# Moving the adjacency's transpose into the last stage of a two-layer decoder, with 47 blocks of rows and a woven last shared expert

## The chip, the cores and the metric

The kernel runs on one core of one Trainium2 chip. A core has TensorE (PE: matrix products, with its weight loads, PEld, beside them), VectorE (DVE), ScalarE (ACT), GpSimd (POOL) and SyncE (SP, which here only issues transfers). The DMA queues carry data between device memory (DRAM) and the on-chip memory (SBUF); PE writes into PSUM banks, from which DVE and ACT read. The metric is device time in microseconds (us), median over several runs of one launch.

## The reference

The input `x` holds 4 batches of 512 tokens with 512 dimensions; a context holds 4 x 512 rows of 128. Two layers follow one another, each step with a residual and a layernorm (all float32):

- layer 0: causal self-attention (16 heads of 32); cross-attention to the context (32 query heads of 16, 8 key heads); a feed-forward net with activations quantised to 8 bits and ternary weights;
- layer 1: causal self-attention; a mix with a learned adjacency; a mixture of experts.

The adjacency comes from the context alone, and is 512 x 512 for each batch:

```python
sim = jnp.einsum('bhnd,bhmd->bnm', Q, K) / (jnp.sqrt(jnp.float32(d)) * H)
k = max(1, int(n * TOP_K_RATIO))                       # 153 of 512
threshold = jax.lax.top_k(sim, k)[0][:, :, -1:]
A_learned = jax.nn.sigmoid(sim) * (sim >= threshold)
A_learned = (A_learned + jnp.swapaxes(A_learned, -1, -2)) * 0.5
return (1.0 - gamma) * adj_raw + gamma * A_learned     # adj_raw is the decoder's x here
```

The mixture of experts sends each of the 2,048 tokens to 2 of 16 experts (512 -> 256 -> 512 with silu and a gate), weights the two results, and adds one shared expert (512 -> 512 -> 512) that all tokens pass:

```python
for e in range(N_EXPERTS):
    h = jax.nn.silu(flat @ Wu[e]) * (flat @ Wg[e])
    out = out + combine[:, e:e + 1] * (h @ Wd[e])
out = out + jax.nn.silu(flat @ Su[s]) * (flat @ Sg[s]) @ Sd[s]
```

## The kernel before

Tokens lie on the 128 partitions: a batch is `X[b]`, 128 x 4 x 512 (NT = 4 tiles of rows). `ident` is the identity matrix, with which PE transposes 128 x 128 pieces into PSUM. The stages follow one another; times are those of the profile:

- 0 to 562 us: self-attention of layer 0. 562 to 1100: cross-attention. 1100 to 1400: feed-forward. 1400 to 1996: self-attention of layer 1. From 1973 on, overlapping its end: `experts`.

**Self-attention and the selection beside it.** In `self_attention` PE's instructions are chained in the order in which they are written (`in_order`, recorded at L424 for all of them; the adjacency's own lines keep their numbers). Between heads it calls `background()`, which advances a generator, `selecting(...)`, by one step. It computes the similarities of a batch (PE products L959 and L964, scaled into SBUF), finds each row's threshold (the 153rd largest) by repeated counting, and then runs `adjacency(b, s, pool)`, L986: a first loop makes the masked half-sigmoid of each row tile (ACT L990, DVE L991 and L993, all in place in the similarity tile `s[i]`), a second loop transposes four pieces per row tile into one PSUM bank (L999), adds the untransposed tile (DVE, L1001), and stores the sum into the DRAM tensor `mixed` (SP, L1002). Layer 0's self-attention carries batches 0 and 1, layer 1's carries 2 and 3. PSUM there is `psum(3, 1, 1)`: three pairs of banks, one bank for transposes (`psum_tp`), and one more. So a transpose group waits until the bank's last reader, a DVE or ACT instruction, is done.

**Cross-attention and the ternary weights.** `cross_attention` runs 135 passes of its inner loop. It calls `background()` in the passes after 2 x NT, and in the passes t = 1, 3, 5, 7, 9, 11 besides; every second call advances the ternary quantisation of the feed-forward weights by one step (51 steps: a load on SP, L681, with DVE work such as L687 behind it). The first passes also issue three DMAs on SP that zero `xs` (L659).

**Experts.** Here no order is pinned: the scheduler of the language orders each engine's instructions from the order of emission and its own estimates. PSUM is `psum(2, 2, 2)`: two pairs, two banks for transposes, two more.

1. For each batch: `mix_adjacency(b, ap)` loads the four row tiles of `mixed` (two buffers `adj`) and adds them to the scaled residual on DVE (L1117); `layernorm` (L105 statistics, L106, ACT root L108, L110, L112 scaling); `transposed` makes `xT` (PE L122, copies on DVE L126 and ACT L124, 16 transposes per batch); `route(b)` does the router (PE L1171, L1179, a chain of small DVE operations L1180 to L1215, ACT's exponent L1188).
2. Counts over all tokens (PE, L1258 to L1269), a chain on DVE that turns them into a position for each (token, choice), and 32 POOL scatters (L1318) that write the rows of `X` into `xs` in DRAM, sorted by expert and padded to blocks of 128 rows.
3. `shared(b, acc)`: in two halves, up and gate products (PE L1226), silu (ACT L1231), product `sh` (DVE L1232), down products (PE L1237) and DVE additions (L1243) into `acc[b]`. It is emitted for batches 0 to 2 after the scatters, and the scheduler puts much of it into PE's gaps of steps 1 and 2; batch 3 is emitted after the blocks (L1384).
4. Blocks: 16 rounds of 3 streams (`LS` = 16, `NS` = 3), block j = s x 16 + k. Each loads its expert's weights on SP if they are new in its stream (L1344, L1349), its 128 rows `xb` (L1353, three buffers), transposes them (L1358, copy L1360), and runs the products (L1363, silu L1368, `h` L1370, transposes L1373, copy L1375, down L1377, copy L1382, store into `ys` on ACT's queue L1383). At most `NB` = 47 blocks can be filled; all 48 of the 3 x 16 run.
5. Return: for each tile of tokens two POOL gathers from `ys` into `yg` (L1390, four buffers), weighted and added on DVE (L1394); then `layernorm` of the batch and its store (SP, L1399).

Of the kernel before, what the change touches and what calls it, by code (L numbers as in the profile page):

```python
# [13 lines left out]
F32 = mybir.dt.float32  # L14
# [3 lines left out]
ALU = mybir.AluOpType  # L18
# [3 lines left out]
P = 128  # L22
B, S, D = 4, 512, 512
NT = S // P
# [16 lines left out]
def decoder_kernel(ctx: ExitStack, tc: tile.TileContext, a: dict, out: bass.AP):  # L41
    nc = tc.nc
    V, A, G, T = nc.vector, nc.scalar, nc.gpsimd, nc.tensor
# [17 lines left out]
    def psum_tp(dt=F32, n=4):  # L61
        return ps["tp"].tile([P, n, P], dt, tag="tp", name="tp")
# [5 lines left out]
    ident = const.tile([P, P], F32, tag="ident", name="ident")  # L68
# [22 lines left out]
    for b in range(B):  # L91
        xb = const.tile([P, NT, D], F32, tag=f"x{b}", name=f"x{b}")
# [7 lines left out]
    def layernorm(b, x=None):  # L100
        x = X[b] if x is None else x
        st = small.tile([P, NT, 6], F32, tag="bst", name="bst")
        mv = small.tile([P, NT, 2], F32, tag="bmv", name="bmv")
        for i in range(NT):
            V.bn_stats(st[:, i, :], x[:, i, :])  # L105
            V.bn_aggr(mv[:, i, :], st[:, i, :])  # L106
        sd = small.tile([P, NT], F32, tag="bsd", name="bsd")
        A.activation(sd, mv[:, :, 1], AF.Sqrt, bias=eps_t)  # L108
        rs = small.tile([P, NT], F32, tag="brs", name="brs")
        V.reciprocal(rs, sd)  # L110
        for i in range(NT):
            V.tensor_scalar(  # L112
                x[:, i, :], x[:, i, :], mv[:, i, 0:1], rs[:, i : i + 1],
                ALU.subtract, ALU.mult,
            )
# [358 lines left out]
    def cross_attention(background):  # L474
        HD, NG, NJ, NP = XD, XG, 4, XP
        multiply, transpose = in_order()
        with tc.tile_pool(name="ck", bufs=1) as kp, tc.tile_pool(
            name="cx", bufs=2
        ) as xp, tc.tile_pool(name="cpt", bufs=3) as pt, tc.tile_pool(
            name="co", bufs=2  # L480
# [5 lines left out]
            for k in range(2):  # L486
                KS.append(kp.tile([P, NG, S], BF16, tag=f"ks{k}", name=f"ks{k}"))
                KL.append(kp.tile([P, NG, S], BF16, tag=f"kl{k}", name=f"kl{k}"))
                t = kp.tile([P, NT, NG, 32], F32, tag=f"va{k}", name=f"va{k}")
                V.memset(t, 1.0)  # L490
                VA.append(t)
            for k in range(3):
                t = kp.tile([P, NT, NJ, 32], BF16, tag=f"xl{k}", name=f"xl{k}")
# [137 lines left out]
            p = o = end = None  # L631
            for t in range(NT * total + 7):
                (n, i), k, v = divmod(t, NT), t - 5, t - 6
                if n < total:
                    maxima(n, i, 0)
                late, p = p, softmax(*divmod(k, NT)) if 0 <= k < NT * total else None
                if late:
                    if v % NT == 0:
                        o = psum_mm()
                    values(*divmod(v, NT), o, late)  # L640
                    if v % NT == NT - 1:
                        end = finish(v // NT, o)
                        next(end)
                if n < total:
                    maxima(n, i, 1)
                if i == 0 and 0 < n <= total:
                    least(n - 1)
                elif i in (1, 2) and n + 1 < total:
                    turn(n + 1, i - 1)
                elif i == 3:  # L650
                    next(end, None) if end else None
                    if n + 2 < total:
                        split(n + 2)
                if t > 2 * NT:
                    background()
                if t < 12 and t % 2:
                    background()
                if i == 0 and 0 < n <= NS:
                    nc.sync.dma_start(  # L659
                        xs[ts(n - 1, LS * P), :].rearrange("(j p) d -> p j d", p=P),  # L660
                        zero.unsqueeze(1).to_broadcast([P, LS, D]),
                    )
# [316 lines left out]
    rest = const.tile([P, 1], F32, tag="rest", name="rest")  # L979
# [4 lines left out]
    mixed = tc.dram_tile([B * NT * P, S], F32, name="mixed")  # L984

    def adjacency(b, s, pool):  # L986

        for i in range(NT):
            e = pool.tile([P, S], F32, tag="y", name="y")
            A.activation(e, s[i], AF.Tanh, scale=0.5)  # L990
            V.tensor_scalar(e, e, quarter, quarter, ALU.mult, ALU.add)  # L991
            n = b * NT + i
            V.scalar_tensor_tensor(s[i], s[i], thr[:, n : n + 1], e, ALU.is_ge, ALU.mult)  # L993
            if i % 2:
                yield
        for i in range(NT):
            tp = psum_tp()
            for c in range(NT):
                T.transpose(tp[:, c, :], s[c][:, ts(i, P)], ident)  # L999
            u = pool.tile([P, S], F32, tag="y", name="y")  # L1000
            V.tensor_tensor(u, tp.rearrange("p c t -> p (c t)"), s[i], ALU.add)  # L1001
            nc.sync.dma_start(mixed[ts(b * NT + i, P), :], u)  # L1002
            if i % 2:
                yield

# [104 lines left out]
    def mix_adjacency(b, ap):  # L1110
        u = ap.tile([P, NT, S], F32, tag="adj", name="adj")
        nc.sync.dma_start(
            u, mixed[b * NT * P : (b + 1) * NT * P, :].rearrange("(t p) d -> p t d", p=P)
        )
        for i in range(NT):
            x = X[b][:, i, :]
            V.scalar_tensor_tensor(x, x, rest, u[:, i, :], ALU.mult, ALU.add)  # L1117
        layernorm(b)


# [5 lines left out]
    NB = (2 * B * S + NE * (P - 1)) // P  # L1126
    NS = 3
    LS = -(-NB // NS)
    NBP = NS * LS

    def experts(xs, ys):
        with tc.tile_pool(name="sims3", bufs=1) as sp:
            select_again(Similarities(sp))
        with tc.tile_pool(name="mx", bufs=1) as xp:
# [82 lines left out]
            def shared(b, acc):  # L1217

                for half in range(2):
                    h = xp.tile([P, F // P, S], F32, tag="sh", name="sh", bufs=2)  # L1220
                    for f in range(F // P):
                        col = ts(half * (F // P) + f, P)
                        pp = psum_pair()
                        for j, w in enumerate((swu, swg)):
                            for c in range(NK):
                                T.matmul(  # L1226
                                    pp[:, j, :], w[:, c, col], xT[b][:, c, :],
                                    start=(c == 0), stop=(c == NK - 1),
                                )
                        s = xp.tile([P, S], F32, tag="ss", name="ss", bufs=2)  # L1230
                        A.activation(s, pp[:, 0, :], AF.Silu)  # L1231
                        V.tensor_tensor(h[:, f, :], pp[:, 1, :], s, ALU.mult)  # L1232
                    for k in range(NT // 2):
                        po = psum_pair()
                        for i in range(2):
                            for f in range(F // P):
                                T.matmul(  # L1237
                                    po[:, i, :], h[:, f, ts(2 * k + i, P)],
                                    swd[:, half * (F // P) + f, :],
                                    start=(f == 0), stop=(f == F // P - 1),  # L1240
                                )
                        two = slice(2 * k, 2 * k + 2)
                        V.tensor_tensor(  # L1243
                            acc[:, two, :], po, (acc if half else X[b])[:, two, :], ALU.add
                        )

            with tc.tile_pool(name="adj", bufs=2) as ap:
                for b in range(B):
                    mix_adjacency(b, ap)
                    t = xp.tile([P, NK, S], F32, tag=f"xT{b}", name=f"xT{b}")  # L1250
# [72 lines left out]
                        tc.declare_no_dep(d.ins, e.ins, reason="rows of their own")  # L1323
                    sent.append(d)
            for b in range(3):
                shared(b, acc[b])

            with tc.tile_pool(name="mw", bufs=1) as wp, tc.tile_pool(name="mh", bufs=3) as hp:
                wug = [wp.tile([P, NK, 2, F], F32, tag=f"wug{s}", name=f"wug{s}") for s in range(NS)]
# [2 lines left out]
                for k in range(LS):  # L1332
                    for s in range(NS):
                        j = s * LS + k

                        with tc.issue_after(last.ins) if last else nullcontext():
                            e = nc.sync.value_load(ebi[0:1, j : j + 1], min_val=0, max_val=NE - 1)
# [43 lines left out]
                        yb = hp.tile([P, D], F32, tag="yb", name="yb")  # L1381
                        A.copy(yb, pp[:, 1, :])  # L1382
                        nc.scalar.dma_start(ys[ts(j, P), :], yb)  # L1383
                shared(B - 1, acc[B - 1])  # L1384
                for b in range(B):
                    for i in range(NT):
                        t = b * NT + i
                        for k in range(2):
                            y = hp.tile([P, D], F32, tag="yg", name="yg", bufs=4)
                            G.indirect_dma_start(  # L1390
                                out=y, out_offset=None, in_=ys,
                                in_offset=bass.IndirectOffsetOnAxis(pos[k][:, t : t + 1], 0),
                            )
                            V.scalar_tensor_tensor(  # L1394
                                acc[b][:, i, :], y, wt[k][:, t : t + 1], acc[b][:, i, :],
                                ALU.mult, ALU.add,
                            )
                    layernorm(b, acc[b])
                    nc.sync.dma_start(out[b].rearrange("(t p) d -> p t d", p=P), acc[b])  # L1399

    xs = tc.dram_tile([NBP * P, D], F32, name="xs")
    ys = tc.dram_tile([NBP * P, D], F32, name="ys")


    def selecting(batches, pool, before=()):
# [96 lines left out]
```

## Time and profile before

| | us |
|---|---|
| median of 3 runs (2554.65 to 2563.09) | 2555.62 |
| profiled execution, device time | 2553.13 |
| its span | 2551.4 |
| PE busy in the span | 2270.9 (89%) |
| DVE busy | 1431.1 (56%) |
| ACT busy | 1102.6 (43%) |
| POOL busy | 625.4 (25%) |
| counts done (PE) | 2041.8 |
| scatters | 2051.2 to 2093.4 |
| first block's products | 2169.3 |
| last product of the blocks | 2474.2 |
| first gather | 2482.3 |

1.7 us of the execution lie outside the span. A line of a group gives the source line, the engine, the operation and its tiles, the number of instructions, and their time. A row of the timeline gives start, length, engine and line, and in brackets how long the engine stood idle before it and whose end released it; rows of PE overlap a little, as its ends are modelled, so the time from one start to the next is the better measure of what an instruction takes. Idle time on an engine that does not bound a stage costs nothing there.

### The profile page before, as it was taken

To read this page: it belongs to the slowest core of one execution; us is meant where nothing else is said; L and a number is where in the kernel's file an instruction comes from. 1 tells how busy PE (TensorE), PEld (TensorE's weight loads), DVE (VectorE), ACT (ScalarE), POOL (GpSimd) and SP (SyncE) were. 2 spreads that over 40 slices of the span, in tenths; PEclk is the share of its full clock that TensorE was granted. 3 is DMA by queue.
4 is the path that set the end of the run, shared out by engine and by line. 5 is a ranking of instruction groups with operands and counts; after the bars stand their busy time and mean duration, and the time that the engine had idled before them with its cause. 6 is when DMAs were issued, how large, how long until landed. Compare 5 with 4: busy or idle time off the path is not lost. (4 is left out here: it accounts for less than half of the span.)

```text
span 2551.4 us, 34801 instructions
## 1 busy us (share of the span) xinstructions
PE 2270.9 (89%) x13032; PEld 1005.0 (39%) x13032; DVE 1431.1 (56%) x3138; ACT 1102.6 (43%) x1742; POOL 625.4 (25%) x1218
## 2 busy tenths in 40 slices
PE   7899889978989899989988689988999889999995
PEld 2334333333333233346555234433434334444442
DVE  2455555548888778758888445555555921111117
ACT  0732373225767677766665273246223200222211
POOL 7300020013333233136766240012000040000004
PEclk9899989889999999999999789998998999999997
DMA  6500000028221301000000200000001260434545
GB/s 220 155 1 18 17 1 1 1 72 308 83 83 53 114 17 34 1 1 1 1 1 1 85 1 1 1 17 1 1 1 53 83 222 17 145 119 155 179 123 186
DMA packets 93725, 164.27 MB, mean 64 GB/s; under 512 B 7408, under 2 KB 39536, under 8 KB 93552
## 3 DMA queue, kind: packets, MB, share of 16 engines
q1 hardware_dynamic: 76144, 123.20, 14.8%
q10 hardware_dynamic: 12288, 22.03, 2.3%
q0 software_dynamic: 5120, 16.78, 2.0%
q8 instruction: 103, 1.69, 0.3%
q14 instruction: 70, 0.57, 0.1%
HBM read 165.13 MB, written 51.90 MB: 85 GB/s over the span
## 5 line engine op out<-in xcount | busy, mean ns | idle before, releaser
L554 DVE TENSOR_REDUCE nm<-sc 128x2 f32<-128x1024 f32 x256 | 304.0, 1218 | 94.5 <-PE sc L424 94.0
L592 ACT ACTIVATE p<-sc 128x1024 f32<-128x1024 f32 x256 | 248.6, 1025 | 128.9 <-PE sc L424 128.7
L246 DVE CUSTOM_DVE_ANT_0 e<-sc,late_keys 128x256 bf16<-128x256 f32 (+3 forms) x512 | 223.3, 485 | 130.2 <-PE sc L424 130.1
L296 ACT ACTIVATE p<-sc 128x512 f32<-128x512 f32 (+3 forms) x256 | 166.0, 701 | 227.3 <-PE sc L424 227.2
L424 PE MATMUL mm<-p,va 128*32 128x512 f32 (+3 forms) x2048 | 215.1, 524 | 0.4 <-ACT oT L607 0.3
L1363 PE MATMUL sc<-wug,xbT 128*128 128x512 f32 x384 | 186.3, 599 | 14.9 <-ACT sl L1368 11.9
L424 PE MATMUL sc<-qs,ks 128*128 128x512 bf16 x512 | 147.4, 381 | 26.8 <-DVE nm L554 25.0
L424 PE MATMUL sc<-kT,qT 32*128 32x512 f32 (+3 forms) x1024 | 136.5, 501 | 25.0 <-ACT p L296 20.9
L424 PE MATMUL sc<-ks,qs 128*128 128x512 bf16 x512 | 155.3, 387 | 3.8 <-DVE nm L554 2.5
L324 DVE RECIPROCAL u<-u 128x128 f32<-128x128 f32 x128 | 108.4, 909 | 68.0 <-ACT u L311 68.0
L424 PE MATMUL sc<-qT,kT 32*128 32x256 f32 (+3 forms) x1024 | 130.8, 507 | 12.6 <-DVE st L246 10.8
L1390 POOL DMA_INDIRECT yg<-ys,pi x32 | 33.2, 1037 | 413.7 <-DMA ys<-yb 390.6
L1032 ACT ACTIVATE junk<-sim,mid 128x512 bf16<-128x512 f32 x176 | 125.2, 726 | 19.3 <-POOL mid L1025 19.3
L747 POOL TENSOR_TENSOR y<-z 128x512 f32<-128x512 f32 (+1 forms) x48 | 97.3, 2040 | 87.4 <-DVE z L732 87.3
L1360 DVE COPY xbT<-tp 128x512 f32<-128x512 f32 x48 | 32.9, 688 | 124.3 <-PE tp L1358 117.4
L1370 DVE TENSOR_TENSOR h<-sc,sl 128x256 f32<-128x256 f32 x48 | 20.2, 420 | 143.7 <-ACT sl L1368 143.7
L1363 PEld LDWEIGHTS sc<-wug,xbT 128*128 128x128 f32 x384 | 67.3, 190 | 81.7 <-issue 64.7
L424 PEld LDWEIGHTS sc<-kT,qT 32*128 32x128 f32 x1024 | 52.4, 189 | 115.1 <-issue 70.2
L747 POOL TENSOR_TENSOR z<-y 128x512 f32<-128x512 f32 x64 | 95.3, 1510 | 3.4 <-issue 2.1
L424 PEld LDWEIGHTS <-ks 128*128 128x128 bf16 x512 | 50.0, 98 | 104.3 <-issue 58.3
L1377 PE MATMUL sc<-wd,hT 128*128 128x512 f32 x192 | 90.2, 592 | 0.0
L424 PEld LDWEIGHTS sc<-qT,kT 32*128 32x128 f32 x1024 | 51.0, 193 | 92.7 <-issue 62.1
(297 smaller groups left out, 4202.5 us busy)
## 6 DMA issues: line engine op xcount, KB each, us to landing
wug<-in_Wu SPq DMA_DIRECT2D x48, 512.0 KB
wug<-in_Wg SPq DMA_DIRECT2D x48, 512.0 KB
wd<-in_Wd SPq DMA_DIRECT2D x48, 512.0 KB
xs<-zero SPq DMA_DIRECT2D x3, 4096.0 KB
xb<-xs SPq DMA_DIRECT2D x48, 256.0 KB
ys<-yb ACTq DMA_DIRECT2D x48, 256.0 KB
w<-in_w_gate SPq DMA_DIRECT2D x16, 512.0 KB
w<-in_w_up SPq DMA_DIRECT2D x16, 512.0 KB
```

The costliest lines, as they stand in the source:

```text
L246: V.tensor_tensor_reduce(e, at[r], late_keys[:, (NT - m) * P :], 1.0, LOWEST, ALU.add, ALU.max, accum_out=st[:, i, r : r + 1],)
L296: A.activation(heads, sc[h][:, :, :m], AF.Exp)
L324: V.reciprocal(sums[:, ts(i, P)], sums[:, ts(i, P)])
L424: ins = op(*args, **kw)
L554: V.tensor_reduce(NM[n][:, i, 2 * h : 2 * h + 2], sc, AX.X, ALU.max, negate=True)
L592: A.activation(p[:, 2 * h : 2 * h + 2, :], sc[h], AF.Exp)
L747: then(pool, getattr(G, op)(*args))
L1032: A.activation(e, s[k], AF.Sign, bias=bias[:, k : k + 1], accum_out=to[:, k : k + 1])
L1360: V.tensor_copy(xbT, tp)
L1363: T.matmul(pp[:, 0, :], xbT[:, c, :], wug[s][:, c, :, :].rearrange("p q f -> p (q f)"), start=(c == 0), stop=(c == NK - 1),)
L1377: T.matmul(pp[:, 1, :], hT[:, c, :], wd[s][:, c, :], start=(c == 0), stop=(c == F // P - 1),)
L1390: G.indirect_dma_start(out=y, out_offset=None, in_=ys, in_offset=bass.IndirectOffsetOnAxis(pos[k][:, t : t + 1], 0),)
```

## The change

- `cross_attention` no longer calls `background()` in the passes t = 1, 3, ..., 11.
- `adjacency` stores the masked tile `s[n]` itself into `mixed`, as soon as it is made. The second loop with its 64 transposes (over the four batches), 16 DVE additions and two yields per batch goes.
- `mix_adjacency` transposes the loaded tiles: 4 transposes per row tile (64 in all) into `psum_tp`, and one more DVE addition that reads them from PSUM (16 in all).
- `shared` becomes a generator that yields after each column of `sh` and each pair of down products (8 yields). For batches 0 to 2 it is run through at once. For batch 3 it is advanced once for two of every three token tiles between the gathers, and run to its end ahead of the last batch's gathers.
- The block loop skips j = 47, the last turn of its third stream; `ys` has 47 x 128 rows.
- The gathered rows use in turn the buffers `yg`, `xb` and `yb`, three each.

```diff
--- before.py
+++ after.py
@@ -653,8 +653,6 @@
                 if t > 2 * NT:
                     background()
-                if t < 12 and t % 2:
-                    background()
                 if i == 0 and 0 < n <= NS:
                     nc.sync.dma_start(
@@ -991,15 +989,7 @@
             V.scalar_tensor_tensor(s[i], s[i], thr[:, n : n + 1], e, ALU.is_ge, ALU.mult)
-            if i % 2:
-                yield
-        for i in range(NT):
-            tp = psum_tp()
-            for c in range(NT):
-                T.transpose(tp[:, c, :], s[c][:, ts(i, P)], ident)
-            u = pool.tile([P, S], F32, tag="y", name="y")
-            V.tensor_tensor(u, tp.rearrange("p c t -> p (c t)"), s[i], ALU.add)
-            nc.sync.dma_start(mixed[ts(b * NT + i, P), :], u)
+            nc.sync.dma_start(mixed[ts(n, P), :], s[i])
             if i % 2:
                 yield
@@ -1113,8 +1103,12 @@
         for i in range(NT):
+            tp = psum_tp()
+            for c in range(NT):
+                T.transpose(tp[:, c, :], u[:, c, ts(i, P)], ident)
             x = X[b][:, i, :]
             V.scalar_tensor_tensor(x, x, rest, u[:, i, :], ALU.mult, ALU.add)
+            V.tensor_tensor(x, x, tp.rearrange("p c t -> p (c t)"), ALU.add)
         layernorm(b)
@@ -1230,6 +1224,7 @@
                         V.tensor_tensor(h[:, f, :], pp[:, 1, :], s, ALU.mult)
+                        yield
                     for k in range(NT // 2):
@@ -1243,6 +1238,7 @@
                             acc[:, two, :], po, (acc if half else X[b])[:, two, :], ALU.add
                         )
+                        yield
@@ -1323,7 +1319,8 @@
             for b in range(3):
-                shared(b, acc[b])
+                for _ in shared(b, acc[b]):
+                    pass
@@ -1332,6 +1329,8 @@
                         j = s * LS + k
+                        if j == NB:
+                            continue
@@ -1381,12 +1380,19 @@
-                shared(B - 1, acc[B - 1])
+
+                rest = shared(B - 1, acc[B - 1])
                 for b in range(B):
+                    if b == B - 1:
+                        for _ in rest:
+                            pass
                     for i in range(NT):
                         t = b * NT + i
+                        if t % 3 != 2:
+                            next(rest, None)
                         for k in range(2):
-                            y = hp.tile([P, D], F32, tag="yg", name="yg", bufs=4)
+
+                            y = hp.tile([P, D], F32, tag=("yg", "xb", "yb")[(2 * t + k) % 3], name="yg")
@@ -1399,7 +1405,7 @@
-    ys = tc.dram_tile([NBP * P, D], F32, name="ys")
+    ys = tc.dram_tile([NB * P, D], F32, name="ys")
```

## Prediction

> **What bounds the kernel now.** I read the engine totals first, then busy time by stage, then the instructions that the diff touches, and last the waits around them on TensorE (PE), VectorE (DVE) and the gather queue (POOL).
>
> The first block is the page's busy line; the second is busy time by stage (columns: window, its length, then PE, PE weight load, DVE, ACT, POOL busy with instruction counts, granted clock, DMA share, GB/s).
>
> ```profile
> PE 2270.9 (89%) x13032; PEld 1005.0 (39%) x13032; DVE 1431.1 (56%) x3138; ACT 1102.6 (43%) x1742; POOL 625.4 (25%) x1218
> ```
>
> ```profile
> core 0: us, PE busy (x) PEld busy (x) DVE busy (x) ACT busy (x) POOL busy (x), PEclk, DMA share, GB/s
> 0.00:560.00 560.00, 500.94 (x3189) 207.41 (x3190) 279.00 (x823) 214.54 (x421) 96.32 (x320) 0.95 0.15 49
> ...
> 1400.00:1973.00 573.00, 509.03 (x3281) 216.52 (x3282) 290.55 (x839) 230.03 (x442) 85.13 (x292) 0.92 0.05 16
> 1973.30:2000.00 26.70, 16.51 (x59) 6.57 (x51) 26.70 (x59) 2.54 (x5) 0.58 (x3) 0.90 0.56 182
> 2000.00:2041.80 41.80, 41.80 (x177) 19.23 (x178) 36.57 (x190) 17.48 (x26) 0.00 (x0) 0.94 0.11 39
> ...
> 2169.45:2474.15 304.70, 285.64 (x839) 134.73 (x838) 48.85 (x93) 63.12 (x141) 0.00 (x0) 1.00 0.46 147
> 2474.15:2551.40 77.25, 47.77 (x103) 20.34 (x101) 49.26 (x93) 11.34 (x16) 33.17 (x32) 0.80 0.54 170
> ```
>
> PE bounds both self-attentions (89% busy) and the blocks (94%). The mixing stage is bound by DVE first (26.70 of 26.70) and then by PE (41.80 of 41.80). In the last 77 us no engine is full: gathers, DVE and PE wait for one another.
>
> The DVE add that follows the adjacency's transposes, with the waits behind it; then PE rows (start, length, work, idle before it and its releaser); then two gathers:
>
> ```profile
> L1001 DVE TENSOR_TENSOR y<-tp,sim x16: 648/692/693, 273.1 to 1951.3; 128x512 f32<-128x512 f32 x16
> ...
>   PEld tp L999: 7.3, 9
>   PE tp L424: 7.1, 4
>   PEld L424: 6.0, 2
> ```
>
> ```profile
> 277.71 0.46 PE L424 MATMUL tp<-ident,pm 128*128 128x128 bf16 x4 [2.00 <-DVE y L1001]
> ...
> 2096.28 1.33 PE L1358 MATMUL tp<-ident,xb 128*128 128x128 f32 x5 [10.89 <-DMA xb<-xs]
> ...
> 2494.92 8.78 PE L1237 MATMUL sc<-swd,sh 128*128 128x512 f32 x14 [4.08 <-DVE sh L1232]
> ```
>
> ```profile
> 2530.97 1.01 POOL L1390 DMA_INDIRECT yg<-ys,pi  x1 [5.77 <-DVE x L1394]
> 2534.73 1.21 POOL L1390 DMA_INDIRECT yg<-ys,pi  x1 [2.76 <-DVE x L1394]
> ```
>
> The reader is to see that L999 stands in PE's written order with one transpose bank, so that PE attention work waits for a DVE add; and that late gathers wait for buffers.
>
> **The change part by part**, against the profiled execution's own 2553.13 us (span 2551.40).
>
> *Self-attention loses 64 transposes and 16 adds.* PE rows around L999, next start minus start, give 2.44, 2.35, 2.08 and 3.2 us of work for the four batches: 10.1. The waits for L1001 are 2.00 + 1.36, 0.97, 2.35 and 1.36 + 0.15: 8.2. What PE gains is lost again where another engine is late next, the softmax's ACT or DVE. PE is busy 0.89 of these stages, so I count 0.89 of the work, 9.0, and two thirds of the waits, 5.5: **-14.5**. Bounds: -18.3 if all is kept, -5 if half the work alone is. The 16 stores stay on SP and go out earlier, right after each mask. The next batch overwrites the similarity tiles, so a late store could hold it; but the masks of a batch are made up to a hundred us ahead (L993 starts at 130, the transposes at 266), so this costs nothing. If that cover went, it would cost one store's landing, about 5 us by the adjacency's load (1987.73 to 1992.79), per batch. Two yields fewer per batch bring the next batch's selection two background calls forward on DVE, ACT and POOL, which changes their work's place and not its amount.
>
> *Cross-attention loses six background calls* (three weight steps and their loads: on SP the first two loads now stand behind two zeroings of `xs`, before one led them at 564.69 and SP stood 9.05 at the next, 567.00; `xs` is first needed at the scatters, 2051, the context's next loads at 607, so SP is no loser). One L687 step of 1.21 us at 582.32 stands in a stretch where DVE runs without a gap (573.1 to 586) and PE then idles 4.47 for DVE (586.39). The steps come back later, where PE is the bound and the 51 steps still end by pass 110 of 135. **-1**; bounds -3 (one DVE step each) and +2 (the three come back exposed, less the first).
>
> *The mixing stage gains 64 transposes, 16 adds from PSUM and table loads.* I walked the new order of PE, DVE and ACT with rows of before: transpose start to start 0.11 to 0.14, L1117 0.65, add 0.60 (L1001 start to start), statistics 0.59 + 0.09, scaling 0.46, copy of xT 0.60, the router's products 3.54. Batch b's mix transposes stand behind batch b-1's x transposes, and both use the same two PSUM banks. The routes end 2026.2, 2044.8 and 2064.9 for batches 1 to 3 (before: 2015.8, 2026.1, 2034.6), and the counts 30.0 later than 2041.8. But 24 more of the shared expert's products (24 x 0.858, each two passes of 0.43 = 20.6) now stand ahead of the counts and leave the stretch behind the scatters. Net +9.4: 48 of the transposes at 0.13 (6.2; the other 16 fit between the Wo groups), one wait of 4.4 of a shared product for `sh` (made at about 2036 behind the mixing on DVE), less 1.4 that batch 0's layernorm gains. That wait also costs clock: 14 products at 0.43 are 6.2 with the last one's end, and L1237 took 8.78 after an idle 4.08 and 7.78 (2097.40) after 10.89, so 1.6 to 2.6 more; I take 2.0, between them. **+11.4**. Bounds: +5 (transposes alone, less the 1.4) and +19 (16 adds exposed as well, 9.6). A gain is excluded: PE is busy 41.80 of 41.80 where most of this is put.
>
> [...]
>
> *47 blocks.* Steady blocks take 6.50 (2303.08 to 2329.06 for four), the first five 5.45, as their rows were transposed while PE waited. A block less is not 6.5 less: in the new order 15 row transposes (3.75 blocks) are made ahead of the first products, not 20 (five blocks), and from the 19th block on each block has one transpose of its successor and three of the one after in its gap. With products at 0.43, transposes at 0.11, and the waits last product to first of 1.43, 1.32 and 1.10 for four, three and one transpose between, the walk gives 302.6 before (trace: 304.9) and 299.2 after: **-3.4**. Bounds -6.5 and +2 (rows arrive late in some blocks: on a block that loads weights the rows' load lands 6.8 after the block's start and is wanted at 6.6).
>
> *Last expert woven, nine buffers instead of four.* Gathers run at 1.37 each when nothing holds them (first ten from 2482.26 = T). Before, they wait 16 us in all for buffers, 5.77 and 2.76 of it near the end, the last issues at T+55.3, and the last scaling L112 ends T+63.7. With nine buffers the last could issue at T+42.5, and landing (3.71, 2537.57 to 2541.28) and finish (4.66) would give T+50.9. DVE denies part of that: in its new order two `sh` stand behind up to seven gathered adds (0.66 each), L1237 waits for them, and the last batch's adds wait for L1237 and the two adds L1243 (1.22 each). The walk ends at T+56.9: **-6.8**. Bounds -12 (the gathers alone) and -2 (L1237 waits as before, 4.08 and 6.09). SP's output stores follow their batches as before; the gathers stay alone on POOL.
>
> *Sum:* -14.5 - 1 + 11.4 - 3.4 - 6.8 = -14.3, so 2553.1 - 14.3 = 2538.8 profiled. The median of the runs is 2555.62, 2.5 above the profiled execution, so I say **2541**.
>
> **Rivals.**
> - *Slower: the mixing stage goes serial.* Place: batch b's mix transposes (two banks) behind b-1's x transposes, with DVE full. My walk spaces the batches (2064.9 - 2026.2)/2 = 19.4 apart. With no overlap a batch is DVE 4 x (0.65 + 0.60 + 0.68 + 0.46) + 2 x 0.60 + about 5.0 of routing (2027.3 to 2033.5 less two other operations) = 15.8; PE 2.1 + 2.1 + 3.8; ACT about 5 (root 0.30, copy 0.57, exponent 0.26, three table loads of 1.28): 28.8. Three intervals 9.4 longer are +28: 2538.8 + 28 = 2567 profiled, 2569. It decides from 26.7 a batch ((14.3 + 7.7)/3 more). For it: DVE's 26.70 of 26.70. Against: the shared expert's products can fill PE's waits and are then not owed later.
> - *No difference: self-attention's time isn't PE's.* Only -5 comes there: -4.8 in all, 2551. For it: 11% of those stages PE waits on softmax. Against: the L1001 waits are followed by PE work at once.
> - *More gained:* all 18 in attention, +5 in the mix, -12 at the end: -18 - 1 + 5 - 3.4 - 12 = -29.4, so 2526. For it: gathers ran unheld for ten in a row. Against: DVE's order in the last stage.
> - *The 4.4 wait costs no clock:* the 2.0 falls away, 2536.8 profiled, 2539. For it: PE went on at full rate after idles of 2.35 and less. Against: the row with 4.08. [...]
> - *The 47th block saves nothing* (the diff doesn't do what it says for time): -10.9, so 2545. Some rhythm is lost for sure.
>
> **How the numbers follow.** Forecast 0.35 (own range 2532 to 2549, which holds the next too), no clock lost 0.15, serial mix 0.14, no difference 0.16, more gained 0.15, no block saved 0.05. 0.3% is 7.7 us, about what a measurement can tell here. Faster: 0.35 + 0.15 + 0.15 + 0.05 = 0.70; same 0.16; slower 0.14. The range 2522 to 2562 reaches past the larger gain (2526) and over no difference (2551) toward the serial mix, and leaves out that one and the far ends: no more than 0.2. All bounds added would be 2521 (-18.3 - 3 + 5 - 6.5 - 12 = -34.8) and 2572 (-5 + 2 + 19 + 2 - 2 = +16).
>
> **What would show it.** In the profile after: no PE wait for the adjacency's add in 0 to 560 and 1400 to 1973, and `experts` reached about 14 earlier; counts then about 16 later than 2041.8 (30 + 2 - 15.5), the scatters' end the same, and the shared products behind them about 20.6 shorter; blocks 47 in about 299 to 302; the last gather by T+50 and the last scaling by T+57. I am wrong if attention's stages hold their lengths, if counts end later than 2081, or if L1237 in the last stage waits more than 10 us for `sh`.

## The result, and the profile after

The changed kernel takes 2532.37 us (median of 4 runs, 2524.9 to 2535.93) beside 2559.05 for the kernel before, timed with it (4 runs): a ratio of 0.9898, 95% interval 0.9868 to 0.9929. Timed once more with the last group of experiments, it took 2541.06 beside 2556.56: 0.9939 (0.9923 to 0.9956). The profiled execution took 2533.2, with a span of 2531.5, 19.9 less than before's 2551.4.

The busy line of the page, and busy time by stage (columns as before: window, its length, then PE, PE weight load, DVE, ACT, POOL busy with counts, granted clock, DMA share, GB/s). The windows begin and end at the same instructions as the stages of before: self-attention of layer 0 and of layer 1, mixing up to the counts in two windows, scatters, the shared expert behind them, blocks, last stage.

```profile
PE 2260.5 (89%) x13014; PEld 1000.8 (40%) x13014; DVE 1426.0 (56%) x3136; ACT 1108.3 (44%) x1744; POOL 630.8 (25%) x1218
```

```profile
0.00:544.00 544.00, 494.00 (x3158) 204.10 (x3159) 273.16 (x815) 214.34 (x421) 97.44 (x320) 0.95 0.15 50
1389.60:1947.30 557.70, 495.95 (x3250) 210.12 (x3252) 286.13 (x831) 230.10 (x442) 85.83 (x292) 0.94 0.05 16
1947.60:1973.30 25.70, 18.17 (x74) 8.56 (x67) 25.12 (x50) 2.35 (x4) 0.58 (x3) 0.92 0.40 130
1973.30:2050.00 76.70, 71.91 (x273) 34.74 (x274) 52.20 (x220) 24.84 (x34) 0.00 (x0) 0.92 0.12 41
2050.00:2104.30 54.30, 42.64 (x98) 18.15 (x97) 15.38 (x43) 2.94 (x5) 30.99 (x32) 0.95 0.67 250
2104.30:2156.13 51.83, 51.80 (x126) 23.80 (x127) 10.78 (x12) 2.39 (x4) 0.00 (x0) 0.95 0.08 22
2156.13:2459.50 303.37, 280.66 (x827) 132.16 (x826) 47.05 (x91) 61.77 (x138) 0.00 (x0) 1.00 0.46 148
2459.50:2531.50 72.00, 47.03 (x102) 19.84 (x100) 48.38 (x93) 11.34 (x16) 35.84 (x32) 0.86 0.58 181
```

Layer 0's attention ends 16 us sooner, and PE's 41.80 full microseconds before the counts have become 76.70, not quite full. The stretch from the first row transposes to the first block, 73.0 before (2096.28 to 2169.29), is 51.8 long.

Rows of PE (start, length, work, idle before it and its releaser). The first stands where 2.00 us were lost to the adjacency's add; the next two are the wait that the prediction's walk had found for `sh`, and the wait for the rows:

```profile
277.52 0.40 PE L424 MATMUL tp<-ident,pm 128*128 128x128 bf16 x4
...
2011.37 2.08 PE L1232 MATMUL sc<-swd,sh 128*128 128x512 f32 x2 [4.30 <-DVE sh L1226]
...
2104.31 1.33 PE L1357 MATMUL tp<-ident,xb 128*128 128x128 f32 x5 [10.69 <-DMA xb<-xs]
```

Late gathers on POOL. None of the 32 waits longer than 0.31 any more; the last starts 44.3 after the first (55.3 before):

```profile
2503.18 3.50 POOL L1396 DMA_INDIRECT yg<-ys,pi  x1 [0.30 <-issue]
...
2511.99 0.95 POOL L1396 DMA_INDIRECT yg<-ys,pi  x1 [0.30 <-issue]
```

Both kernels run the same products in a written order up to `experts`, so their traces can be laid beside each other product by product. The 19.9 come out as follows (the marks, at their times before: first output projection of layer 0 204.1; its last 561.0; first Hadamard product 1112.4; first query product of layer 1 1446.4; last value product 1974.5; first scatter 2051.2; first block 2169.3; first gather 2482.3; end):

| us, against the profiled execution before | forecast | changed kernel | the same once more |
|---|---|---|---|
| up to the first mark | | -1.6 | -1.7 |
| self-attention, layer 0 | | -14.5 | -13.2 |
| self-attention, layer 1 | | -14.3 | -15.6 |
| both | -14.5 | -28.8 | -28.8 |
| cross-attention | -1 | +5.8 | +7.5 |
| feed-forward | | -1.0 | -1.3 |
| last value product to first block | +11.4 | +12.5 | +14.2 |
| first block to first gather | -3.4 | -1.5 | -2.4 |
| first gather to end | -6.8 | -5.3 | -1.5 |
| sum | -14.3 | -19.9 | -14.0 |

### The profile page after: what moved, and what is told of

Its sections match the earlier page's. It is cut to its first block, busy times and chain, and to the rows that moved or that the text cites. A ratio compares the mean times of both kernels' runs of the same rounds, so it can differ in the third digit from the quotient of the medians.

```text
span 2531.5 us, 34777 instructions
## 1 busy us (share of the span) xinstructions
PE 2260.5 (89%) x13014; PEld 1000.8 (40%) x13014; DVE 1426.0 (56%) x3136; ACT 1108.3 (44%) x1744; POOL 630.8 (25%) x1218
## 5 line engine op out<-in xcount | busy, mean ns | idle before, releaser
L1362 PE MATMUL sc<-wug,xbT 128*128 128x512 f32 x376 | 185.1, 600 | 16.8 <-ACT sl L1367 13.6
L424 PE MATMUL sc<-qT,kT 32*128 32x256 f32 (+3 forms) x1024 | 134.1, 509 | 17.4 <-DVE st L246 15.6
L424 PEld LDWEIGHTS sc<-kT,qT 32*128 32x128 f32 x1024 | 51.8, 189 | 114.7 <-issue 73.6
L742 ACT ACTIVATE g<-sc,sg 128x512 f32<-128x512 f32 x64 | 43.8, 685 | 93.9 <-PE sc L733 62.2
```

What stands on the lines that cost most here:

```text
L424: ins = op(*args, **kw)
L742: then(act, A.activation(*args, **kw))
L1362: T.matmul(pp[:, 0, :], xbT[:, c, :], wug[s][:, c, :, :].rearrange("p q f -> p (q f)"), start=(c == 0), stop=(c == NK - 1),)
```

## The experiments

Runs of one group were timed on one chip, beside the kernel before. One theory runs through them, that the sum has the parts of the table and that each belongs to the edit to which the prediction gave it. The rivals are that attention's surplus and cross-attention's loss are the scatter of single executions, or belong to other edits.

### The adjacency moved, alone

```diff
-                T.transpose(tp[:, c, :], s[c][:, ts(i, P)], ident)
-            u = pool.tile([P, S], F32, tag="y", name="y")
-            V.tensor_tensor(u, tp.rearrange("p c t -> p (c t)"), s[i], ALU.add)
-            nc.sync.dma_start(mixed[ts(b * NT + i, P), :], u)
+            nc.sync.dma_start(mixed[ts(n, P), :], s[i])
...
+                T.transpose(tp[:, c, :], u[:, c, ts(i, P)], ident)
...
+            V.tensor_tensor(x, x, tp.rearrange("p c t -> p (c t)"), ALU.add)
```

> The kernel before with the adjacency and mixing parts of the change alone. The changed kernel's trace, set beside that of before product by product, gains 28 us inside the two self-attentions (16.1 by the end of layer 0, of which 1.6 at the very start; about 15 in layer 1) and gives 12.5 back between the end of attention and the first block. Theory A (all of this belongs to the move): 28 - 12.5 = 15 faster, ratio 0.994, the gains again in four places: where each batch's transposes stood, and just behind those of batches 0 and 2. Theory B (the 10 beyond the 18.3 that I priced are luck of that one execution's clock or belong to another part): 18.3 - 12.5 = 6 faster, 0.998.

2542.4 beside 2553.59: 0.9949 (0.9934 to 0.9963), about 13 us. In the trace the attentions gain 13.5 and 12.5, and the way from the last value product to the first block is 14.0 longer. So the surplus over 18.3 is no luck of one execution: theory A. The time alone lies between the two theories' 15 and 6, as the blocks take 4.3 longer in this form (see "47 blocks alone"). Four kernels with the adjacency as before show how far the attentions scatter: -2.8, +0.7, +5.9 and +0.7 against the profiled execution before; seven with the move, and no dead work in its place, gained 26.0 to 30.1.

### The move with the two yields put back

To the kernel with the adjacency moved alone, behind the loop of `adjacency`:

```diff
             if i % 2:
                 yield
+        yield
+        yield
```

> The same, with the two yields per batch put back behind the stores (two steps of selection that do nothing), so that the next batch's selection starts as late as before. If the gain beyond the priced 18.3 comes from the selection's start being two calls earlier, this is 8 to 10 us slower than the mixing parts alone, and the stretches behind batches 0 and 2 (290 to 375 and 1690 to 1775) gain nothing. If the extra is what the freed bank and the waits' end bring by themselves, the two agree within 4 us.

2544.1: 0.9958 (0.9943 to 0.9972), not to be told from the one without; the attentions gain 16.8 and 10.0. The selection's earlier start is not the source.

### The move with the transposes kept as dead work

In the same place:

```diff
             if i % 2:
                 yield
+        for i in range(NT):
+            tp = psum_tp()
+            for c in range(NT):
+                T.transpose(tp[:, c, :], s[c][:, ts(i, P)], ident)
+            if i % 2:
+                yield
```

> The mixing parts alone, but the 64 transposes of the adjacency stay in self-attention too, as work that nobody reads: no add, no wait for one. It tells PE's work from the waits and DVE's adds. With the prices of my prediction 10.1 of the 18.3 are work and 8.2 waits: 9 to 10 slower than the mixing parts alone (ratio 0.9949 there, so 0.9987), the attentions gaining 17 to 18 of their 27. If the gain is mostly the waits and the clock that they cost, 3 to 6 slower.

2556.28 beside 2552.92: 1.0017 (1.0004 to 1.003), 17 us more than the move alone by the ratios (0.0068 of 2553), and 15 more than the form with the yields put back (0.0059), which is the nearer one, as this edit keeps two yields per batch as well. The attentions gain 8.8 and 2.2, 11.0 of some 28. So 64 transposes cost 15 to 17 us where they stood, with nobody waiting for an add: some 0.25 each, not the 0.14 that I had taken (9.0 of 64, after the discount).

### The move with the adds kept as dead work

In the same place:

```diff
             if i % 2:
                 yield
+        for i in range(NT):
+            u = pool.tile([P, S], F32, tag="y", name="y")
+            V.tensor_tensor(u, s[(i + 1) % NT], s[i], ALU.add)
+            if i % 2:
+                yield
```

> The mixing parts alone, but 16 adds of that size stay on DVE in self-attention (of two similarity tiles, read by nobody), with no transposes and no PE work that waits for them. 16 x 0.69 = 11 us of DVE. If DVE's time there is hidden, as I counted it, within 2 us of the mixing parts alone. If the part of the gain that I did not price is DVE time in PE's chain, 5 to 9 slower.

2544.92: 0.9959 (0.9943 to 0.9974), attentions -14.7 and -10.9. The adds are some 11 us of DVE (16 x 0.69), and the attentions gain 25.6 with them, 26.0 without: DVE's time for them is hidden here. What PE lost to the adds of before is its waits for them, 8.2 by the rows.

The granted clock says where some of the surplus lies. Two windows in each of three kernels, behind the adjacencies of batches 0 and 2 (columns as above; the clock stands third from the end). Before:

```profile
240.00:400.00 160.00, 144.32 (x886) 59.65 (x887) 85.93 (x250) 79.99 (x168) 24.36 (x128) 0.94 0.02 7
1640.00:1790.00 150.00, 135.17 (x825) 55.44 (x824) 80.13 (x226) 73.44 (x162) 29.15 (x132) 0.92 0.02 8
```

The changed kernel:

```profile
240.00:400.00 160.00, 151.63 (x983) 61.30 (x982) 89.54 (x264) 80.73 (x171) 25.30 (x128) 0.97 0.02 8
1640.00:1790.00 150.00, 135.80 (x901) 56.12 (x900) 84.29 (x236) 77.27 (x166) 29.85 (x132) 0.97 0.03 9
```

With the transposes kept:

```profile
240.00:400.00 160.00, 148.04 (x978) 61.10 (x976) 87.91 (x256) 80.92 (x171) 24.35 (x128) 0.96 0.02 8
1640.00:1790.00 150.00, 137.55 (x860) 57.27 (x856) 79.15 (x230) 75.44 (x164) 29.16 (x132) 0.93 0.02 8
```

0.03 of 160 and 0.05 of 150 are about 12 us of clock, near the surplus of 10 over 18.3. With the transposes kept it is 3 and 1.5.

The whole of both attentions can be split in this way. The time between two marks of the table above is PE's idle time plus its busy time. Where the trace has the clock at half, I count half of the busy time as the cost of the clock, an estimate from rows like those below (four products in 3.61 and 3.63 at half, in 1.94 at full clock); the rest counts as work at full rate. (Ends on PE are modelled, so a part is good to a few us.) Against the kernel before:

| us, both attentions | whole | PE idle | cost of half rate | work at full rate |
|---|---|---|---|---|
| changed kernel | -28.8 | -9.2 | -13.0 | -6.6 |
| the same once more | -28.8 | -9.9 | -11.5 | -7.4 |
| adjacency moved, alone | -26.0 | -9.6 | -9.1 | -7.3 |
| transposes kept | -11.0 | -9.1 | -2.0 | +0.1 |

So work and waits give what was priced, and what lies beyond the 18.3 is granted clock. In the eight executions with the move and no transposes kept, the cost of half rate is 6.1 to 13.8 lower than before; in the four with the adjacency as before it differs by -1.4 to +6.0, which is its scatter. (With the yields put back, and with the adds kept, the split puts 13.0 and 11.4 on work, so a single part shouldn't be pressed.) Two rows of the kernel before show half rate at work. They stand behind the waits of 2.00 (at 277.71) and 2.35 for the adjacency's add, and products of the same form come a few us later at full rate:

```profile
277.96 3.61 PE L424 MATMUL mm<-L0wv,xt 128*128 128x512 f32 x4
282.23 1.94 PE L424 MATMUL mm<-L0wv,xt 128*128 128x512 f32 x4
...
1680.48 0.40 PE L424 MATMUL tp<-ident,pm 128*128 128x128 bf16 x4 [2.35 <-DVE y L1001]
1680.71 3.63 PE L424 MATMUL mm<-L1wv,xt 128*128 128x512 f32 x4
1685.00 1.94 PE L424 MATMUL mm<-L1wv,xt 128*128 128x512 f32 x4
```

Two windows at the first of them, the 3.40 us that the clock is at half and as much ahead of them (PE busy in the second figure, the clock third from the end):

```profile
274.50:277.90 3.40, 1.40 (x12) 0.50 (x11) 2.16 (x6) 0.00 (x0) 0.00 (x0) 1.00 0.21 77
277.90:281.30 3.40, 3.40 (x8) 1.18 (x5) 0.97 (x4) 0.59 (x1) 0.00 (x0) 0.50 0.21 77
```

The granted clock is at half (0.50) from 277.9 to 281.3, and PE was busy for 1.40 of the 3.40 us ahead of it, its longest wait there being the 2.00. Behind the wait of 2.35 it is 0.51, from 1680.7 to 1684.2. So in these two places half rate follows a wait for the adjacency's add; that the wait causes it is inferred from the rows. It can't be the only cause: with the transposes kept no product waits for an add, PE's idle time falls as in the other forms (-9.1), and yet only 2.0 of clock come back. What else the clock answers to there stays open.

### Cross-attention's early calls removed, alone

```diff
-                if t < 12 and t % 2:
-                    background()
```

> The kernel before without the six early background calls of cross-attention, and nothing else. My prediction says 1 us faster; the changed kernel's trace loses 5.5 us between the end of layer 0's self-attention and the end of cross-attention (16.1 ahead at 549, 10.7 ahead at 1088). If that loss is the removed calls': 5 slower, ratio 1.002, with about the same loss in the same stage. If it is the scatter of single executions: within 2 us.

2566.48: 1.0046 (1.003 to 1.0063), some 12 slower. The profiled execution, the fastest of its six, loses 4.0 in cross-attention and 5.4 in the feed-forward stage, where PE waits twice for the gated product `h` of DVE, 2.9 and 3.0 us instead of 0.65 and 1.52 (at 1139.86 and 1144.66 before). The edit changes no line of that stage, the changed kernel doesn't show it (0.64 and 1.52), and what made `h` late stays open. So 4 of the 12 are in the edit's own stage.

### The changed kernel with those calls put back

```diff
+                if t < 12 and t % 2:
+                    background()
```

> The changed kernel with the six early background calls put back. By the loss theory it is 5 us faster than the changed kernel (ratio to before 0.988 where that had 0.990); by the scatter theory it is within 2 us of it.

2535.89: 0.9928 (0.9909 to 0.9946). The changed kernel had 0.9898 and, once more, 0.9939, so the time doesn't tell them apart. The stage does, mostly: without the calls cross-attention is 4.0, 4.2, 5.8 and 7.5 longer than before, with them -0.9 to +1.7 in eight kernels, and +5.1 in a ninth (the one with rows later and calls back). PE's waits in the stage (who waited for whom, us in total, times, longest), before and after:

```profile
PE sc L424 <- DVE nm L554: 26.5, 23, 3.9
```

```profile
PE sc L424 <- DVE nm L554: 27.6, 23, 4.0
```

The first gap is shorter, as forecast (4.47 at 586.39 before, 3.47 at 569.27 after). One of 3.98 comes at 712.32, in a head that before had none. So some of the steps that were put off fall into heads where PE waits for DVE's maximum `nm`, but these waits grow by 1.1 in all. Split as above (from the last output projection to the first Hadamard product), the 5.8 of the changed kernel are 0.7 of idle time, 5.7 of granted clock and -0.6 of work, and the 4.0 of the form without the calls alone are -0.2, 4.6 and -0.4. Forms with the calls lose clock too against that execution of before (-0.2 to +7.6), but have 0.9 to 3.0 less idle time where the trace has all of PE's records. So why the stage is longer without them stays open.

### 47 blocks alone

```diff
                         j = s * LS + k
+                        if j == NB:
+                            continue
```

> The kernel before with 47 blocks alone. My walk says -3.4 (ratio 0.9987); a whole block's rhythm would be -6.5 (0.9975); the changed kernel's trace shows -1.4 from the first product to the first gather, by which it would be 0.9995. Which of them the span from first product to first gather shows (313.0 before) tells more than the time.

2546.37 beside 2552.92: 0.997 (0.9958 to 0.9982). First block to first gather takes 306.0 instead of 313.0: a whole block, 7.0. But with the adjacency moved and all 48 blocks that stretch was 317.3, 4.3 longer than before. One difference is in the row transposes made ahead of the first block. Before:

```profile
2096.28 1.33 PE L1358 MATMUL tp<-ident,xb 128*128 128x128 f32 x5 [10.89 <-DMA xb<-xs]
2119.61 0.71 PE L1358 MATMUL tp<-ident,xb 128*128 128x128 f32 x5
2141.03 0.71 PE L1358 MATMUL tp<-ident,xb 128*128 128x128 f32 x5
2162.46 0.71 PE L1358 MATMUL tp<-ident,xb 128*128 128x128 f32 x5
```

With the adjacency moved, and nothing else:

```profile
2106.99 1.27 PE L1354 MATMUL tp<-ident,xb 128*128 128x128 f32 x5
2128.86 0.71 PE L1354 MATMUL tp<-ident,xb 128*128 128x128 f32 x5
2150.29 0.71 PE L1354 MATMUL tp<-ident,xb 128*128 128x128 f32 x5
```

The mixing stage now uses up shared products that used to stand between the scatters and the blocks, and the scheduler makes one group of row transposes fewer among those left. That group alone isn't the 4.3: the third block's last down product starts 1.1 later (19.5 after the first block's start, 18.4 before), and with rows transposed later (below) two groups stand ahead, and the stretch is 310.9 all the same, where the changed kernel has 311.5. The rest comes later in the loop, whose row transposes are ordered otherwise throughout; that this order is the cause is argued, not shown by a run of its own. 4.3 - 7.0 = -2.7; my walk's -3.4 had both in one number.

### The woven expert with nine buffers, and the buffers alone

The first has all lines of the change from `shared` to the return; the second only these:

```diff
-                            y = hp.tile([P, D], F32, tag="yg", name="yg", bufs=4)
+                            y = hp.tile([P, D], F32, tag=("yg", "xb", "yb")[(2 * t + k) % 3], name="yg")
```

> The kernel before with the woven last expert and the nine buffers alone. Walk: -6.8 (0.9973). The changed kernel's trace from first gather to end has 63.9 where before has 69.1: -5.3 (0.9979). If the last stage gains less without the other parts, above 0.999.

> The kernel before with nine buffers for the gathered rows, the last shared expert where it was. The woven form with nine buffers gained 7.1 from first gather to end (69.1 to 62.1 there) and 11 in the time. If the buffers do it: the last stage 6 to 8 shorter here too, ratio 0.996 to 0.998. If the weave does it: gathers issue early but the last stage is within 2 of before, as DVE's adds of the last batch still wait for the expert's products.

Both together: 2545.42, 0.9957 (0.994 to 0.9974). The buffers: 2551.79, 0.998 (0.9969 to 0.9992). First gather to end: 62.1 and 65.4, beside 69.2 before. The last gather starts 42.5 and 44.5 after the first (55.3 before), so the buffers alone free the gathers. They bring 3.8 of 7.1, between what the two expectations said, and the weave, or the scatter between two executions, the rest. The whole time of the woven form fell by 11, four more than its last stage shows in a profiled execution that was the slowest of its six (2551.67, the others 2539.08 to 2549.76).

### The changed kernel once more, and rows transposed later

The changed kernel as it is; with the first round's row transposes ordered behind the last up or gate product of batch 2's first half (below); and with that order and cross-attention's six calls.

```diff
+                                if b == 2 and half == 0:
+                                    ups.append(up.ins)
...
+                            d = T.transpose(tp[:, c, :], xb[:, ts(c, P)], ident)
+                            if k == 0:
+                                tc.add_manual_dep(d.ins, ups[-1].name, ORDER, reason="after shared")
```

> The changed kernel itself once more, beside its two relatives on one chip: 0.990 as before. Its cross-attention should again be 4 to 6 longer than before's; if that was one execution's scatter, within 2 of it.

> The changed kernel, with the first round's row transposes held behind the shared expert's 32 up and gate products of batch 2's first half, so that PE doesn't stand still for the rows' landing (10.7 us at 2104.31 in the changed kernel, 10.9 before). Only the order on PE changes. If the shared products are what PE could do there: 10.7 less, about 1 given back as fewer rows are transposed ahead of the first block, so 9 to 10 faster than the changed kernel. If the rows' late transposes hold up the blocks as much: within 2 of it.

> The same with the six early background calls of cross-attention put back. If their removal costs what the traces show (4 to 5 in cross-attention), 4 to 5 faster than the one without; if not, within 2.

On one chip: the changed kernel 2541.06, 0.9939 (0.9923 to 0.9956); rows later 2543.94, 0.9957 (0.9944 to 0.997); with the calls back as well 2540.67, 0.9933 (0.9916 to 0.9949). Nothing is gained. PE no longer waits for rows there, but it waits in the same place, for `sh`. PE, then ACT, of the kernel with the rows later:

```profile
2102.72 8.71 PE L1236 MATMUL sc<-swd,sh 128*128 128x512 f32 x16 [13.18 <-DVE sh L1230]
```

```profile
2101.34 1.09 ACT L1229 ACTIVATE ss<-sc 128x512 f32<-128x512 f32 x2 [32.59 <-remote]
```

The products that this silu reads were all issued by 2082.1 and 2089.0, and ACT had nothing else to do. The trace records PE's semaphore, for which the silu waits, at 2101.32, and knows no instruction that ended there ("remote"). The same kernel without the new order sometimes shows it too (below), hidden behind the rows' wait. No version here is faster than the changed kernel beyond the intervals.

## Why the prediction was right, and where it was not

The forecast of 2541 with a range of 2522 to 2562 holds both results, 2532 and 2541, and the sign is right. Term by term it is less good than the sum.

- *Self-attention, -14.5 with -18.3 as its end:* measured -28.8, twice as much and outside the bound. The place and the mechanism hold: the wait at 277.71 is gone. By the split above work fell by 6.6 and 7.4 (9.0 counted) and idle time by 9.2 and 9.9 (5.5 counted): together 15.8 and 17.3, inside the bounds. The step that failed is a term put at nothing: granted clock in these stages, 13.0 and 11.5. The prediction reads that "PE went on at full rate after idles of 2.35 and less"; the rows behind 2.00 and 2.35 show half rate (3.61 and 3.63 for four products, not 1.94). The discount for waits that come back elsewhere was wrong too: idle time fell by more than the 8.2 that were priced, so on balance none came back. The price of a transpose from its own row (10.1 for all) was not too low for its work; kept as dead work the 64 cost 15 to 17, about half of it clock (2.0 instead of 9.1 come back).
- *Cross-attention, -1 (-3 to +2):* measured +4 to +7.5, on the wrong side and outside the bounds. The gain at 582 is there, 1 us. The failed step is the price of what comes back, put at DVE steps that PE waits for: in the changed kernel PE's idle time grows by 0.7 only, and 5.7 are granted clock, for which the sum had no term here either. Why the stage is longer without the calls stays open.
- *Mixing, +11.4:* +12.5, and +14.2 once more. The walk's wait of 4.4 for `sh` is there at 4.30, the first scatter 33.9 later against the attention's end (32 by the walk), the shared products behind 21.2 shorter (20.6). With the waits inside it the stage is neither serial nor hidden, so the slower rival and the larger gain both fail here. From 2010.2, within that wait, to 2017.0 the clock is at half, and PE is busy for 5.63 of it: 2.8 us lost, where 2.0 were added, so the rival "the 4.4 wait costs no clock" fails too. (The three pieces of the net 9.4 add up to 9.2.)
- *Blocks, -3.4:* -1.5 and -2.4. The split was -7.0 for the block and +4.3 with the adjacency moved.
- *Last stage, -6.8:* -5.3 and -1.5, -7.1 alone. The gathers were free from the first to the last, as forecast (the last at T+44.3); the adds behind them were held by the expert, and the last scaling ends at T+58.5, not T+56.9.
- *The rivals:* "self-attention's time isn't PE's" is refuted by the kept transposes; "the 47th block saves nothing" by 306.0 beside 313.0.

That the sum came within 5.6 and 0.3 us of two profiled executions is owed to misses of both signs: attention's gain was put 14.3 too low, cross-attention's loss 6.8 to 8.5 too low, and the last stage's gain 1.5 to 5.3 too high. So the number was in part luck: the two largest misses, in the changed kernel mostly clock, have opposite signs.

## What to carry to other kernels

Price work in a written order on the bounding engine by taking it out, or by keeping it dead, and not only by its own rows: here 64 transposes were worth 15 to 17 us where their rows said 10. Read the rows behind a wait as well as the wait: behind 2.00 us PE took 3.61 for products that take 1.94, and this clock was the largest term that the sum lacked. Ask of every edit which filler it uses up: the mixing stage borrowed shared products from the stretch ahead of the blocks, and in that form the blocks took 4.3 longer. Don't call background steps that are put off free: four kernels lost 4.0 to 7.5 where a count of DVE steps said 1 gained.

## What the hardware showed that I had not expected

In some of these executions ACT starts 3 to 19 us late on products that were issued before, while indirect transfers are under way. Commonly a silu of the shared expert starts 0.04 us after its products. In eight of the fourteen profiled executions (the changed kernel's second one among them, not its first) one silu in the scatter stage starts some 19 us late, whatever the kernel, and always 5.5 to 5.7 after the last scatter's start (in the kernel before, the first rows are back on the chip 5.6 after it). It isn't ACT alone: in the same eight DVE idles 6.0 to 9.5 ahead of its second addition of down products there, in the other six 2.2. The row in the changed kernel's second execution, and in its first (a wait for the products only):

```profile
2105.96 1.08 ACT L1225 ACTIVATE ss<-sc 128x512 f32<-128x512 f32 x2 [32.71 <-remote]
```

```profile
2085.93 0.60 ACT L1225 ACTIVATE ss<-sc 128x512 f32<-128x512 f32 x1 [13.96 <-PE sc L1220]
```

The first block comes only 1.7 later against the attention's end (+14.2 instead of +12.5); in the first execution PE stands 10.69 for the rows in this stretch. In the last stage the like is dearer: the last silu's table load follows its products at once in the changed kernel's first execution, 3 us late in the second, and 9 us late in the kernel with rows later and calls back, whose last stage took 73.6. In that kernel:

```profile
2514.03 1.28 ACT L1231 ACT_TABLE_LOAD   x1 [10.63 <-remote]
```

What holds ACT back isn't visible in the trace, nor whether the products themselves end late (their ends are modelled) or only their signal; that the indirect transfers cause it is inferred from the times alone. In these traces it is the largest part of the scatter of the last stage with nine buffers: 9 of the 11.5 us between 62.1 (the woven form alone, where that load follows its products at once) and 73.6. With the rows held back for the shared expert PE waited 13.2 for `sh` in both profiled executions, instead of 10.7 for the rows: the expert was held too, and nothing was gained.
